# A gated cross-attention layer with experts: the shared part of the last twelve token tiles as six further experts in products of quarters

## The chip, the cores and the metric

The kernel runs on one core of a Trainium2 chip, in one launch. The metric is the time of an execution in microseconds of device time; before the change it is 3289.31 us, the median of three runs (3281.03 to 3296.91). The profile is that of one further execution. Everything is float32. TensorE (PE in the profile) multiplies, VectorE (DVE) and ScalarE (ACT) empty its PSUM banks and compute elementwise, GpSimd (POOL) computes elementwise and issues gathers and scatters, and SyncE (SP) issues nearly all other transfers.

## The reference, cut to what matters

There are 8 x 512 = 4096 tokens of width 1024, which the kernel takes as 32 tiles of 128 rows.

```python
x = x + tanh(g_xattn) * mlstm(layernorm(x), ctx, ctx, ...)        # 16 heads, causal
y = layernorm(x)
logits = y @ router_w.T                                           # 16 experts
w, idx = top_k(softmax(logits), 2);  w = w / sum(w)
shared = (silu(y @ shared_gate_w) * (y @ shared_up_w)) @ shared_down_w      # hidden width 1024
routed[t] = sum over t's two experts of w * ((silu(y @ gate_w[e]) * (y @ up_w[e])) @ down_w[e])   # hidden width 512
out = x + tanh(g_ffn) * (shared + routed)
```

Every token goes through the shared part, and through two of the sixteen experts.

## The kernel before, in words

The order of the work is the program's: a build step places the instructions on each engine, near the order in which they are written but moved where operands are ready, and each engine then runs its own list strictly in order, waiting on semaphores. SP's list is one of these: a transfer that has to wait for its buffer holds back all that stand behind it.

**Attention, with shared units beside it.** A loop over the 32 tiles (the second half of `flamingo_layer`, from `for i in range(1, NT)`) computes attention for tile i, prepares tile i+1 and finishes tile i-1. `finish_rows` (L663) stores the new row x1 and its layer norm y to DRAM, `turn_rows` (L671) stores y transposed (`yT_d`) and queues the shared part of finished tiles as units. `shared_units` (L218) makes them: eight `chunk` units (L247; a chunk is 128 hidden columns, gate and up, weights streamed by `stream`, 1 MB per chunk), then for each tile two `project_down` units (L269). The first six tiles (SINGLE) are queued one by one, 128 columns per matmul and half the cost of a unit in a chunk; tiles 6 to 25 in pairs, 256 columns. `fill` (L207) pops units at four fixed places of each step, and a fifth time in steps 1 to 27. The result, x1 plus tanh(g) times the shared part, goes to `base_d`.

**Routing.** Each tile's two experts and its places in their lists are found beside attention. After the last tile a chain of small DVE operations orders the experts and makes the lists of tokens (`tok_i`, `row_i`), whereupon POOL gathers the first rows and SP loads the first weights. A branch on the number of overflowing tokens follows (L1123 and L1124; every engine reads the number there).

**Experts.** For each expert (loop over `e`), 512 rows, in ten of them 64 more. Both projections are done in quarters: two by two blocks of weights and rows, seven products in place of eight (the Winograd form), with sums of weights by POOL (`weight_sums`, L1134, four operations of 128 x 512 for a step), sums of rows by DVE (`token_sums`, L1101), and the quarters put together by DVE and ACT as they are read out of PSUM (`Step`, L1168). Each expert has four steps (gate and up, two each), in which `down_sums` (L1207) lets POOL prepare the down weights, and two halves of the down projection (`down_tiles`, L1218), before which DVE forms sums of the hidden values (hsum). The results are scaled by ACT and scattered to `routed_d`, two rows per token. Weights lie in a pool of four buffers (`wts`): `load_hidden` (L1054) and `load_down` (L1065) take a buffer when the matmuls of its last user are through. Six PSUM banks rotate under the products (`bank`, L1153). A pool of five buffers (`gat`) holds gathered rows.

**Tail.** After the last expert the shared part of tiles 26 to 31 is done as three pairs of plain units, with the weights held in SBUF, and beside it POOL adds up all outputs: `combine` (L1296) loads the two routed rows and the base of a tile, adds them with two POOL operations of 128 x 1024 (`add_routed`, L1271), and issues the store itself. For the six last tiles the routed rows are added to x1 first, and DVE adds the shared part half by half and SP stores it (L278, L1302).

Of the kernel before, what the change touches and what calls it, by code (L numbers as in the profile page):

```python
# [35 lines left out]
LAST = 3  # L36
SINGLE = 6
SPARE = 4
SLOTS = 5
# [3 lines left out]
def flamingo_layer(  # L43
# [151 lines left out]
    class Unit:  # L195
        def __init__(self, run, load=None, cost=1.0):
            self.run, self.load, self.cost = run, load, cost
            self.also = None
# [7 lines left out]

    def fill(n: float = 1):  # L207
        while n > 0 and units:
            unit = units.popleft()
            n -= unit.cost  # L210
            unit.ready()
            for k in range(min(2, len(units))):
                units[k].ready()
            unit.run()
            if unit.also is not None:
                unit.also()

    def shared_units(pools, tiles, gate_up, down, store, more=None, near=None):  # L218


# [3 lines left out]

        def new(kind, shape):
            pool, tag, bufs = pools[kind]
            return pool.tile(shape, F32, tag=tag, name="sh_" + kind, bufs=bufs)

        def load_y():
# [3 lines left out]
            st["yT"] = new("yT", [P, NC, 2 * P])  # L233
# [5 lines left out]
        def load_chunk(k: int):  # L239
            if k == 0:  # L240
                load_y()
            st[k] = gate_up(k)
            if k == 2 and more is not None:
                for t in range(len(tiles)):
                    load_row(t)

        def chunk(k: int):  # L247
            if k == 0:
                st["hT"] = new("hT", [P, 2 * NFC, 2 * P])
# [8 lines left out]
            act = new("act", [P, 2 * P])  # L258
# [3 lines left out]
        def load_row(t: int):  # L262
            if ("row", t) not in st:
                st["row", t] = new("base", [P, D])
                nc.sync.dma_start(st["row", t], x1_d[tiles[t]])
                if more is not None:
                    more(tiles[t], st["row", t])

        def project_down(t: int, half: int):  # L269
            cols = slice(half * 512, (half + 1) * 512)  # L270
            po = ps.tile([P, 512], F32, tag="o", name="pso")
            for k in range(2 * NFC):
                nc.tensor.matmul(  # L273
                    po, lhsT=st["hT"][:, k, t * P : (t + 1) * P], rhs=down(k)[:, cols],
# [4 lines left out]
            store(tiles[t], row, half)  # L279
# [22 lines left out]

    sh_pools = {"yT": (sh, "yT2", 2), "hT": (sh, "hT2", 1), "base": (sh, "base", 2), "act": (sh, "act", 2)}

    def keep_base(i: int, row, half: int):
        if half == 1:
            nc.sync.dma_start(base_d[i], row)
# [5 lines left out]
    with ExitStack() as actx:  # L313
# [357 lines left out]
        def turn_rows(i: int):  # L671
# [8 lines left out]
            if (alone or i % 2 == 1) and i < NT - 2 * LAST:  # L680
                tiles = [i] if alone else [i - 1, i]
                near = yT if i == 0 else None
                units.extend(shared_units(sh_pools, tiles, stream, lambda k: sh_down[:, k, :], keep_base, near=near))
# [89 lines left out]
        prep_norm(2)  # L773
        for i in range(1, NT):
            nxt, last, back = i + 1 < NT, i % NS == NS - 1, i > 1
            if nxt:
                prep_queries(i + 1)
                prep_keys(i + 1)
# [3 lines left out]
            fill()  # L782
# [9 lines left out]
            fill()  # L792
# [6 lines left out]
            fill()  # L799
# [12 lines left out]
            fill()  # L812
# [6 lines left out]
            if i < NT - SPARE:  # L819
                fill(SLOTS - 4)  # L820
# [205 lines left out]

    NQ = NC // 2
# [26 lines left out]
    def load_hidden(n: int, pool=wts):  # L1054

        e = n // 2
        if e < NE:
            w = (gate_w, up_w)[n % 2][of_expert(e)].rearrange("o (c p) f -> p (o c) f", p=P)
        else:
            fs = slice((e - NE) * F, (e - NE + 1) * F)  # L1060
            w = (sh_gate_w, sh_up_w)[n % 2][:, fs].rearrange("(c p) f -> p c f", p=P)
        ws[n] = pool.tile([P, NC, F], F32, tag="w", name="w")
        nc.sync.dma_start(ws[n], w)

    def load_down(e: int, pool=wts, tag="w"):  # L1065
        wdn[e] = pool.tile([P, NFC, D], F32, tag=tag, name="wd")
        if e < NE:
            w = down_w[of_expert(e)].rearrange("o (c p) d -> p (o c) d", p=P)
        else:
            w = sh_down_w[(e - NE) * F : (e - NE + 1) * F, :].rearrange("(c p) d -> p c d", p=P)  # L1070
# [29 lines left out]

    def token_sums(e: int):  # L1101
        if e >= NE:
            return
# [10 lines left out]

    fill(len(units) + 1)
    streamed.close()
    tk = ctx.enter_context(tc.tile_pool(name="tk", bufs=1))
    for k in range(NM + 1):
        transpose_rows(0, k)
    token_sums(0)  # L1120
# [8 lines left out]
    hidden = ExitStack()  # L1129
    hd = hidden.enter_context(tc.tile_pool(name="hid", bufs=2, side="right"))  # L1130

    sums: dict = {}

    def weight_sums(g: int):  # L1134

        n, i = g // 2, g % 2
        if n >= 2 * NE:
            return
        w = ws[n]
        a11, a12, a21, a22 = (  # L1140
            w[:, q * NQ : (q + 1) * NQ, (2 * f + i) * P : (2 * f + i + 1) * P] for f in range(2) for q in range(2)
        )
        tile_ = hd.tile([P, 3, NQ, P], F32, tag="s", name="wsum", bufs=2)
        s1, s2, s4 = (tile_[:, k] for k in range(3))
        nc.gpsimd.tensor_tensor(s1, a21, a22, ALU.add)  # L1145
        nc.gpsimd.tensor_tensor(s2, s1, a11, ALU.subtract)  # L1146
        nc.gpsimd.tensor_tensor(a21, a11, a21, ALU.subtract)
        nc.gpsimd.tensor_tensor(s4, a12, s2, ALU.subtract)
        sums[g] = [a11, a12, s4, a22, s1, s2, a21]
# [68 lines left out]
    def down_tiles(e: int, i: int):  # L1218
# [31 lines left out]
        for t in (1, 0):  # L1250
            j = e * NM + i + 2 * t
# [16 lines left out]
    routed = routed_d[0 : 2 * T, :].rearrange("(k t) d -> t k d", k=2)  # L1268
    combined = 0

    def add_routed(i: int, row=None):  # L1271

        nonlocal combined
        if combined % 3 == 2:
            rows = [gt_.tile([P, D], F32, tag="gat", name="sum") for _ in range(3 if row is None else 2)]
            parts = rows[:2]
            for k in range(2):
                nc.sync.dma_start(parts[k], routed[i * P : (i + 1) * P, k, :])
        else:
            if combined % 3 == 0:  # L1280
                t = tk.tile([P, 3, NQ, WIDE // 2], F32, tag="t", name="sums")
                rows = t.rearrange("p k c n -> p (k c n)")[:, : 3 * D].rearrange("p (k d) -> p k d", d=D)
            else:
                rows = tl_[0].tile([P, 3, D], F32, tag="rows", name="sums")
            parts = [rows[:, k, :] for k in range(2)]
            nc.sync.dma_start(rows[:, 0:2, :], routed[i * P : (i + 1) * P])
            rows = [rows[:, k, :] for k in range(3)]
        combined += 1
        if row is None:
            row = rows[2]  # L1290
            nc.sync.dma_start(row, base_d[i])
        for part in parts:
            nc.gpsimd.tensor_tensor(row, row, part, ALU.add)
        return row

    def combine(i: int):  # L1296
        row = add_routed(i)
        nc.gpsimd.dma_start(out_rows[i * P : (i + 1) * P, :], row)

    def store_half(i: int, row, half: int):  # L1300
        cols = slice(half * 512, (half + 1) * 512)
        nc.sync.dma_start(out_rows[i * P : (i + 1) * P, cols], row[:, cols])  # L1302

    def held(k: int):
        cols = slice(k % NFC * P, (k % NFC + 1) * P)
        return tuple(ws[2 * (NE + k // NFC) + n][:, :, cols] for n in range(2))

    tl_ = []
    pools = {"yT": (mx_, "xT", 2), "hT": (mv_, "hT", 1), "base": (mv_, "yo", 3)}
    pairs = [  # L1310
# [80 lines left out]
```

## Time and profile before

| | |
|---|---|
| the profiled execution | 3280.16 us, of which the span of its instructions is 3278.4 us |
| median of three runs | 3289.31 us |
| attention with units | 0 to some 1676 us |
| experts 0 to 15 | 1692.8 to 3026.4 us; with rest rows 85.6 to 86.5 us each, without 76.8, the last 72.5 |
| tail | 3026.4 to 3278.4 us |
| TensorE clock granted | 0.985 on average |
| DMA | 567.55 MB, 173 GB/s on average; 299 GB/s in the tail |

A line of instructions reads: line, engine, operation, output and inputs, shapes, count, then busy time, mean of one in ns, and how long the engine was idle just before these and what ended that. A float32 product of TensorE is two instructions, and the recorded durations of a stream of matmuls overlap, so it is the busy time that adds up. In the list of transfers the last number is the median time from issue to landing.

### The profile page before, as it was taken

What the parts mean: (1) busy time and instruction counts of PE and PEld (TensorE: products, weight loads), DVE (VectorE), ACT (ScalarE), POOL (GpSimd) and SP (SyncE); (2) the same over time, 40 slices, a digit from 0 to 9 for tenths busy, and PEclk for the clock granted to TensorE, in tenths of its full rate; (3) what the DMA queues carried; (4) which work ended last, traced back from release to release, by engine and by line L of the source; (5) the groups of instructions that cost most, each with busy time, mean ns of one, the idle gap of its engine ahead of it and who ended that gap; (6) DMA issues with size and microseconds to landing.
All of it is one profiled execution on the core that took longest, in us unless ns stands there. A gap on an engine that the chain in (4) does not pass through costs nothing. (4 is left out here: it accounts for less than half of the span.)

```text
span 3278.4 us, 44195 instructions
## 1 busy us (share of the span) xinstructions
PE 3190.7 (97%) x17043; PEld 2367.7 (72%) x17043; DVE 1673.5 (51%) x3779; ACT 884.9 (27%) x1830; POOL 1173.9 (36%) x904
## 2 busy tenths in 40 slices
PE   6899999999999999999979999999999999999999
PEld 5788778777877867877846666666666777777776
DVE  5646665566675676667534444444444455543000
ACT  3433443434434434434211111111111111111000
POOL 2211111212111111112145554555555555542685
PEclk8899989999999999999989999999999999999999
DMA  6688776556655655655553333333333343334896
GB/s 199 180 229 256 225 207 185 179 169 180 199 162 174 200 169 173 187 168 168 161 188 113 119 128 136 128 132 132 126 117 127 133 152 137 122 124 143 330 346 223
DMA packets 456680, 567.55 MB, mean 173 GB/s; under 512 B 24016, under 2 KB 343424, under 8 KB 452496
## 3 DMA queue, kind: packets, MB, share of 16 engines
q1 hardware_dynamic: 426784, 477.83, 45.9%
q0 software_dynamic: 26064, 86.04, 7.2%
q8 instruction: 137, 2.24, 0.3%
q10 hardware_dynamic: 3616, 0.79, 0.1%
q14 instruction: 79, 0.65, 0.1%
HBM read 447.72 MB, written 116.88 MB: 172 GB/s over the span
## 5 line engine op out<-in xcount | busy, mean ns | idle before, releaser
L1162 PE MATMUL pq<-xT,w 128*128 128x288 f32 (+1 forms) x1536 | 381.7, 399 | 9.9 <-DVEq L1124 9.9
L254 PE MATMUL pgu<-sh_yT,swg 128*128 128x256 f32 (+1 forms) x1920 | 380.6, 350 | 4.2 <-DMA swg<-L_ffn_shared_gate_w_dram 3.3
L273 PE MATMUL pso<-sh_down,sh_hT 128*128 128x512 f32 x832 | 371.8, 598 | 1.3 <-DVE sh_hT L260 1.3
L254 PE MATMUL pgu<-sh_yT,swu 128*128 128x256 f32 (+1 forms) x1920 | 367.6, 344 | 1.9 <-DMA swu<-n_L_ffn_shared_up_w_dram 1.9
L1162 PEld LDWEIGHTS pq<-xT,w 128*128 128x128 f32 x1536 | 292.7, 191 | 85.7 <-issue 20.7
L254 PEld LDWEIGHTS pgu<-sh_yT,swu 128*128 128x128 f32 x1920 | 317.9, 191 | 35.6 <-DMA swu<-n_L_ffn_shared_up_w_dram 2.5
L254 PEld LDWEIGHTS pgu<-sh_yT,swg 128*128 128x128 f32 x1920 | 311.7, 191 | 40.5 <-DMA swg<-L_ffn_shared_gate_w_dram 2.3
L113 POOL TENSOR_SCALAR ve<-bmv 128x1 f32<-128x1 f32 x64 | 15.6, 243 | 782.6 <-DVE bmv L125 782.6
L273 PEld LDWEIGHTS pso<-sh_down,sh_hT 128*128 128x128 f32 x832 | 153.4, 190 | 174.1 <-issue 167.1
L1162 PE MATMUL pq<-tsum,wsum 128*128 128x288 f32 (+1 forms) x1024 | 261.2, 398 | 12.5 <-POOL wsum L1146 12.5
L260 DVE TENSOR_TENSOR sh_hT<-sh_act,pgu 128x256 f32<-128x256 f32 (+1 forms) x152 | 56.8, 375 | 389.5 <-ACT sh_act L259 389.1
L1162 PEld LDWEIGHTS pq<-tsum,wsum 128*128 128x128 f32 x1024 | 192.1, 191 | 52.9 <-POOL wsum L1146 12.9
L1186 DVE TENSOR_TENSOR hT<-pq,u 128x288 f32<-128x288 f32 (+1 forms) x128 | 57.0, 445 | 275.2 <-PE pq L1162 254.9
L541 POOL TENSOR_SCALAR_AFFINE_SELECT d<-d 128x2048 f32<-128x2048 f32 x31 | 62.9, 2028 | 351.5 <-DMA d<-nm_d 294.7
L259 ACT ACTIVATE sh_act<-pgu 128x256 f32<-128x256 f32 (+1 forms) x152 | 53.3, 351 | 488.9 <-PE pgu L254 481.1
L254 PE MATMUL pgu<-sh_yT,w 128*128 128x256 f32 x768 | 166.2, 379 | 0.0
L1145 POOL TENSOR_TENSOR wsum<-w 128x512 f32<-128x512 f32 x64 | 82.5, 1290 | 225.4 <-PE pq L1162 208.3
L254 PEld LDWEIGHTS pgu<-sh_yT,w 128*128 128x128 f32 x768 | 145.9, 190 | 21.1 <-issue 1.4
L565 ACT ACTIVATE d<-d,cols 128x128 f32<-128x128 f32 x496 | 149.9, 388 | 40.0 <-DVE cols L526 24.3
L1252 ACT ACTIVATE yo<-yo,wslot 128x1024 f32<-128x1024 f32 x64 | 73.5, 1149 | 294.3 <-DVE yo L1237 294.3
L1098 ACT COPY xT<-ptx 128x512 f32<-128x512 f32 (+1 forms) x74 | 41.2, 557 | 393.9 <-PE ptx L1095 386.3
L601 PE MATMUL pav<-v,d 128*128 128x65 f32 x1024 | 142.6, 270 | 1.6 <-ACT sq L607 1.6
(266 smaller groups left out, 5711.3 us busy)
## 6 DMA issues: line engine op xcount, KB each, us to landing
swg<-L_ffn_shared_gate_w_dram SPq DMA_DIRECT2D x128, 512.0 KB, 4.6
swu<-n_L_ffn_shared_up_w_dram SPq DMA_DIRECT2D x128, 512.0 KB, 5.1
w<-in_L_ffn_gate_w_dram SPq DMA_DIRECT2D x16, 2048.0 KB, 10.7
w<-in_L_ffn_up_w_dram SPq DMA_DIRECT2D x16, 2048.0 KB, 9.2
wd<-in_L_ffn_down_w_dram SPq DMA_DIRECT2D x16, 2048.0 KB, 7.8
d<-nm_d SPq DMA_DIRECT2D x31, 1024.0 KB, 6.0
sums<-routed_d SPq DMA_DIRECT2D x22, 1024.0 KB, 6.2
x_sb<-in_x_dram SPq DMA_DIRECT2D x32, 512.0 KB, 5.1
```

Of the source, the lines that this page charges most:

```text
L254: nc.tensor.matmul(pg[:, half, :n], lhsT=w[:, c, :], rhs=st["yT"][:, c, :n], start=(c == 0), stop=(c == NC - 1),)
L259: nc.scalar.activation(act[:, :n], pg[:, 0, :n], AF.Silu)
L260: nc.vector.tensor_mul(st["hT"][:, k, :n], act[:, :n], pg[:, 1, :n])
L273: nc.tensor.matmul(po, lhsT=st["hT"][:, k, t * P : (t + 1) * P], rhs=down(k)[:, cols], start=(k == 0), stop=(k == 2 * NFC - 1),)
L541: nc.gpsimd.affine_select(out=q.d, in_=q.d, compare_op=ALU.is_ge, fill=NEG, base=0, pattern=[[0, NH], [1, P]], channel_multiplier=-1,)
L565: nc.scalar.activation(q.d[:, h, :], q.d[:, h, :], AF.Exp, bias=q.cols[:, 0, h : h + 1])
L601: nc.tensor.matmul(pav[:, 2 * k + hh, :], lhsT=q.d[:, h, :], rhs=q.v[:, h, :], start=first, stop=first or hh == 1,)
L1098: copy(dst[:, half * 4 : half * 4 + 4, :], pt[:, :, cols])
L1145: nc.gpsimd.tensor_tensor(s1, a21, a22, ALU.add)
L1162: nc.tensor.matmul(out, lhsT=left[:, c, :], rhs=right[:, c, :], start=(c == 0), stop=(c == chunks - 1))
L1186: nc.vector.tensor_tensor(out, part, other, ALU.add)
L1252: nc.scalar.activation(rows[t], rows[t], AF.Copy, scale=wslot.pop(j))
```

## The change

`HELD = 3` groups of four tiles (20 to 31) are held back from the units beside attention. Their shared part, 1024 hidden columns, becomes two jobs of 512 for each group, and these six jobs follow the sixteen experts in the same loop (`JOBS = 22`), with the same products of quarters: rows come from `yT_d` by plain loads (`load_rows`) in place of gathers and transposes, the second job of a group uses the sums of the first, and the result is added by DVE to a held tile of four rows (`add_shared`) instead of being scattered; after the second job SP stores it. The three pairs of the tail are gone. The adding up that POOL did beside the tail now stands in the jobs (`sums_beside`): in the first job of each group the routed rows are added to the x1 rows of its four tiles, and the twenty other tiles are combined one at a time; one of the two adds of each tile is DVE's now, the other POOL's, and the parts and the row of a combine lie in the five `gat` buffers.

Beside attention there are 20 tiles for 26, the first two alone, the others in pairs. `fill` carries over what it owes: it runs units while something is owed, at four places of a step, 0.75 of a unit at each in steps 1 to 4 and `each` = 99 / 108 of a unit afterwards, so that 8 units are left for the end of the stage. `weight_sums(0)` is moved ahead of the branch, and `token_sums(0)` behind it.

```diff
-LAST = 3
-SINGLE = 6
-SPARE = 4
-SLOTS = 5
+HELD = 3
+SINGLE = 2
+RESERVE = 8
+FIRST = 4
...
+    owed = 0.0
+
     def fill(n: float = 1):
-        while n > 0 and units:
+        nonlocal owed
+        owed += n
+        while owed > 1e-6 and units:
             unit = units.popleft()
-            n -= unit.cost
+            owed -= unit.cost
...
             alone = i < SINGLE
-            if (alone or i % 2 == 1) and i < NT - 2 * LAST:
+            if (alone or i % 2 == 1) and i < NT - 4 * HELD:
...
+        each = (6 * (NT - 4 * HELD) - 1 - 3 * FIRST - RESERVE) / (4 * (NT - 1 - FIRST))
         for i in range(1, NT):
+            share = 0.75 if i <= FIRST else each
...
-            fill()
+            fill(share)
...
-            if i < NT - SPARE:
-                fill(SLOTS - 4)
...
+    JOBS = NE + 2 * HELD
...
+    def load_rows(q: int):
+
+        x = columns(NE + 2 * q)
+        for t in range(NM):
+            nc.sync.dma_start(
+                x[:, :, t * P : (t + 1) * P], yT_d[held_tile(q, t)].rearrange("p (c t) -> p c t", t=P)
+            )
...
     def token_sums(e: int):
-        if e >= NE:
+        if e >= JOBS:
+            return
+        if e > NE and (e - NE) % 2 == 1:
+            xTs[e, "b"] = xTs[e - 1, "b"]
             return
...
+    weight_sums(0)
     for k in range(NM + 1):
         transpose_rows(0, k)
-    token_sums(0)
     early.close()

     nov = nc.values_load(nov_i, min_val=0, max_val=2 * T)
...
+    token_sums(0)
...
         for t in (1, 0):
+            if e >= NE:
+                add_shared(e, i + 2 * t, rows[t])
+                continue
...
+    def add_routed(i: int, row, base):
+
+        nc.sync.dma_start(row, base[i])
+        for k in range(2):
+            part = gt_.tile([P, D], F32, tag="gat", name="part")
+            nc.sync.dma_start(part, routed_d[k * T + i * P : k * T + (i + 1) * P, :])
+            (nc.vector, nc.gpsimd)[k].tensor_tensor(row, row, part, ALU.add)

     def combine(i: int):
-        row = add_routed(i)
+        row = gt_.tile([P, D], F32, tag="gat", name="row")
+        add_routed(i, row, base_d)
         nc.gpsimd.dma_start(out_rows[i * P : (i + 1) * P, :], row)
...
+    def add_shared(e: int, t: int, part):
+
+        q, half = (e - NE) // 2, (e - NE) % 2
+        row = xTs[NE + 2 * q, "sum"][:, t, :]
+        nc.vector.scalar_tensor_tensor(row, part, tgf, row, ALU.mult, ALU.add)
+        if half == 1:
+            i = held_tile(q, t)
+            nc.sync.dma_start(out_rows[i * P : (i + 1) * P, :], row)
+
+    todo = deque(range(NT - NM * HELD))
+
+    def sums_beside(e: int, k: int):
+
+        if e < NE:
+            return
+        if (e - NE) % 2 == 0 and k < 4:
+            if k == 0:
+                xTs[e, "sum"] = mx_.tile([P, NM, D], F32, tag="xT", name="held")
+            add_routed(held_tile((e - NE) // 2, k), xTs[e, "sum"][:, k, :], x1_d)
+        elif todo:
+            combine(todo.popleft())
+
+    for e in range(JOBS):
+        q = (e + 1 - NE) // 2 if e + 1 >= NE and (e + 1 - NE) % 2 == 0 and e + 1 < JOBS else None
+        if q == 0:
+            load_rows(q)
         for k in range(4):
...
             step.finish()
+            sums_beside(e, k)
+        if q:
+            load_rows(q)
         load_down(e + 1)
...
         down_tiles(e, 0)
         token_sums(e + 1)
-        if e == NE - 1:
-            pairs[0][0].ready()
+        sums_beside(e, 4)
         down_tiles(e, 1)
...
         load_hidden(2 * e + 4)
-
-    hidden.close()
...
-    for pair in pairs:
-        units.extend(pair)
...
-    while units:
-        fill()
-        while todo and len(todo) * n > (len(units) - 6) * (NT - 2 * LAST):
-            combine(todo.popleft())
+        if e < JOBS - 1:
+            sums_beside(e, 5)
```

## The prediction

> **What bounds the kernel now.** I read the busy shares first, then the groups by shape, then windows cut at the stage borders, then TensorE's waits, then the DMA landings.
>
> ```profile
> span 3278.4 us, 44195 instructions
> ...
> PE 3190.7 (97%) x17043; PEld 2367.7 (72%) x17043; DVE 1673.5 (51%) x3779; ACT 884.9 (27%) x1830; POOL 1173.9 (36%) x904
> ```
>
> TensorE is busy for all but 87.7 us, so the span is TensorE's work plus those gaps. The work that the change touches, by shape:
>
> ```profile
> L273 PE MATMUL pso<-sh_down,sh_hT 128*128 128x512 f32 x832 | 371.8, 598 | 1.3 <-DVE sh_hT L260 1.3
> ...
> L254 PE MATMUL pgu<-sh_yT,swg 128*128 128x256 f32 x1280 | 301.0, 386 | 0.0
> ...
> L254 PE MATMUL pgu<-sh_yT,swu 128*128 128x256 f32 x1280 | 289.3, 379 | 0.0
> ...
> L254 PE MATMUL pgu<-sh_yT,w 128*128 128x256 f32 x768 | 166.2, 379 | 0.0
> ...
> L254 PE MATMUL pgu<-sh_yT,swg 128*128 128x128 f32 x640 | 79.5, 277 | 4.2 <-DMA swg<-L_ffn_shared_gate_w_dram 3.3 <-DMA sh_yT<-yT_d 0.8
> L254 PE MATMUL pgu<-sh_yT,swu 128*128 128x128 f32 x640 | 78.3, 275 | 1.9 <-DMA swu<-n_L_ffn_shared_up_w_dram 1.9
> ...
> L273 PE MATMUL pso<-wd,sh_hT 128*128 128x512 f32 x192 | 82.9, 592 | 0.0
> ```
>
> Busy time over count is what an instruction costs in a stream (a float32 product is two instructions): 0.231 us for 256 columns beside attention, 0.216 in the tail, 0.123 for 128 columns, 0.447 and 0.432 for 512. The means (379 and more) overlap and don't add. The windows are attention steps 20 to 27, steps 28 and 29, experts 14 and 15, and the tail:
>
> ```profile
> 1058.30:1461.00 402.70, 399.83 (x2537) 304.32 (x2536) 257.17 (x652) 164.55 (x354) 75.46 (x62) 1.00 0.58 178
> 1461.00:1546.20 85.20, 84.84 (x601) 67.27 (x600) 59.67 (x148) 36.63 (x81) 18.59 (x16) 1.00 0.58 180
> ...
> 2877.10:2953.90 76.80, 76.44 (x313) 56.34 (x312) 38.68 (x66) 12.73 (x23) 34.20 (x25) 1.00 0.35 124
> 2953.90:3026.40 72.50, 72.50 (x282) 53.30 (x281) 26.82 (x58) 10.49 (x19) 22.04 (x16) 1.00 0.38 138
> 3026.40:3278.00 251.60, 248.22 (x961) 182.11 (x959) 19.82 (x37) 10.71 (x26) 166.69 (x92) 1.00 0.81 299
> ```
>
> The columns are length, then busy PE, PEld, DVE, ACT, POOL, then clock, DMA share and GB/s. A step with five shared units lasts 50.3 us (402.7 / 8) with DVE busy 32.1; with four units 42.6, and TensorE is still never short (0.36 us idle in two steps). The gaps sit in the first five steps (31.6 us from 18 to 286 us, timeline), in the change from attention to experts (22.4), the rest scattered.
>
> **Work removed and added.** Beside attention four single tiles and one pair go. A single is 256 instructions x 0.123 + 32 x 0.447 = 45.8 us, a pair 256 x 0.231 + 64 x 0.447 = 87.7: 4 x 45.8 + 87.7 = 271 us. In the tail three pairs go: 166.2 + 82.9 = 249. Added are six jobs of 512 rows and 512 hidden columns in seven products instead of eight. Expert 15 is such a job exactly (no rest rows, no transposes for a follower): 72.5 us, all busy; 56 x 0.216 = 12.1 per step, four steps 48.5, then 24 of down products. 6 x 72.5 = 435. TensorE's work: 435 - 520 = **-85 us**. All of it was on the path. Weight loads (191 ns) lie under products of 0.216, so they cost nothing. ScalarE is at 14% in expert 15 and loses the scaling of rows in the jobs: nothing.
>
> **Attention with fewer units.** From step 5 on, 11 units stand where 12 slots are; fill runs one whenever something is owed, so each third step has three units, with the slot between the second scores and the values empty, and two have four. The four-unit step is in the trace: no new idle. A three-unit step has 14.2 us of attention and 3 x 7.1 of units, 35.6 us, against 32 of DVE plus what DVE waits for in any case (row<-rstd alone 30.4 us in 17 steps, 1.8 each): nearly level, and DVE is in order. I take 3 us of idle in each of nine such steps and 0.6 in the other eighteen, 38, against 15 now: **+20**. Bounds: 0 (DVE catches up in the longer steps) and +66 (3 us in every step). In the first four steps the units fall from 5 to 3 while the clock is half at times: **+5**, bounds 0 and 15.
>
> **From attention to experts.**
>
> ```profile
> PE pq L1162 <- POOL wsum L1146: 12.5, 1, 12.5
> PE pq L1162 <- DVEq L1124: 9.9, 1, 9.9
> ```
>
> After the last routing product (pw at 1656.3 us) TensorE had 46 down instructions as cover; the built program of the changed kernel has 62, so 16 x 0.44 = 7 us more. The first weight sums now stand before the branch at L1124 on POOL; SP passes the branch only when its 8 MB of weights are issued (SP took 11.5 and 12.6 us at two issues), which doesn't change, and the token sums now stand behind it on DVE, 1.4 us for the first: 2.5 us won of 12.5. **-9.5**, bounds -18 and 0.
>
> **The adds inside the jobs.** This part speaks against the change. In the tail POOL did all adds (2.35 us each) and TensorE, DVE and ACT waited for none of it. Now each of 32 tiles has one add on DVE (1.22 us, by the row of L661 of that shape) and one on POOL, and the built order puts them among DVE's evictions and POOL's weight sums. It doesn't spread them: jobs 16 and 18 get four held tiles and eight combines each, job 20 four and four, odd jobs none. Queued behind a waiting DVE add are evictions, hence PSUM banks and the hidden values of the down products; behind a waiting POOL add, the next weight sums. Five buffers carry rows and parts: the first part of combine n+2 takes the row buffer of combine n, so SP issues it when that row's store has landed, and everything behind it on SP waits too.
>
> ```profile
> x_sb<-in_x_dram SPq DMA_DIRECT2D x32, 512.0 KB, 5.1
> ...
> sum<-routed_d SPq DMA_DIRECT2D x20, 512.0 KB, 9.9
> ...
> out_dram<-sums POOLq DMA_DIRECT2D x17, 512.0 KB, 5.2
> ...
> out_dram<-sum POOLq DMA_DIRECT2D x9, 512.0 KB, 7.6
> ```
>
> With 5 us a load and 5.2 a store, from job 16's start (0): the fourth held part gets a buffer after POOL's first held add at 20 and lands at 25; DVE adds it by 26, POOL by 28.6; then weight sums (4 x 1.3) to 34, combine 0's POOL add to 36.3, its store lands at 42, combine 2's part at 47, DVE's add done at 48.2, where three evictions of step 3 have waited since 40. Combine 1's POOL add stands behind further weight sums: 44.3; stored 50; combine 3's part 55; DVE's add 56. It stands before the last evictions of step 3 and the hidden sums (4.3 us): the down products start at 60.3 instead of 48.5, **12 us late**. Combines 4 to 7 then stay just ahead. Jobs 18 and 20 have the same order around combines 2 and 3.
>
> Here the Trainium skill (DMA: Bandwidth & Descriptors, Anatomy of one DMA) prices a POOL-issued DMA at about 2.0 us plus bytes over 436 GB/s: 3.2 us for 512 KB. The row says 5.2. With 3.2 for stores and loads the same walk ends 7 us late; with the loaded pair 9.9 and 7.6, 24 late at combine 3 and 42 by the job's end, as combines 6 and 7 are then late too. Job 16 moves 26 MB, some 300 GB/s, as much as the tail's 299, but its loads are one or two at a time, not in threes as the tail's: I stay nearest the 5 us rows, with 13 a job.
>
> A second rule speaks against gaps like these: TensorE: Matmul & The Clock Gate (Why this matters for your kernels) says that an idle gap over about 3 us brings the half clock back. The trace, after the first gap:
>
> ```profile
> 1692.84 5.85 PE L1162 MATMUL pq<-xT,w 128*128 128x288 f32 x16 [9.94 <-DVEq L1124]
> ...
> 1724.61 4.04 PE L1162 MATMUL pq<-xT,w 128*128 128x288 f32 x16
> ```
>
> 1.8 us lost at this gap; after the other, 2.1 more (8 instructions in 4.21 against 2.10). The rule's single 3.4 us window at half rate would be 1.7. I take 2. So 3 x (13 + 2) = **+45**, bounds 27 and 117.
>
> **The end.** Now one DVE eviction (0.75) and a 256 KB store follow the last product. Then: an eviction, two scaled adds of 1024 (1.3 each) and 512 KB: **+4**, bounds 3 and 8.
>
> **Sum.** -85 + 20 + 5 - 9.5 + 45 + 4 = -20.5. The profiled execution took 3280.2 us (span 3278.4), so 3259.7. The median of the runs, 3289.3, lies 9 above it; I put the forecast half-way, at 3264.
>
> **Rivals.** (a) The adds hardly wait: loads and stores near 3 us (shortest landings 2.6 and 2.0): 7 + 2 a pair of jobs, 27 instead of 45, and attention keeps up: 3222 to 3245. For: one load at a time. Against: the medians. (b) Slower: the chain store, load, DVE add, POOL add, store in jobs 16, 18 and 20 becomes the bound, as loads take 9.9 and stores 7.6: 42 + 42 + 24 + 9 = 117, 3280 - 65.5 + 117 = 3332. It decides from 22 us a pair of jobs on, where -65.5 is used up. For: 26 MB in a job, weights of 2 MB in the same queue. Against: at such latencies the job moves only 230 GB/s, so there's no load to cause them. (c) Attention becomes bound by DVE, 3 us idle in each step: +66 for +20, about 3306. Against: the four-unit steps. That the products would not shrink is excluded: their number is in the built program.
>
> **Chances.** My case 0.45 (3240 to 3285), (a) 0.2, (b) 0.22, (c) 0.13. One half of a per cent, 16 us, is about what a measurement of this kernel can tell from no change. Faster by more: 0.25 of my case and (a), 0.45; within: 0.25; slower: (b) and part of (c), 0.30. The range 3222 to 3335 takes in (a) and most of (b).
>
> **What would show it.** Right: steps of 36 and 43 us; jobs of 72.5 us in 17, 19, 21 and some 85 in 16 and 18; DVE adds waiting for DMA there, TensorE for hidden sums after step 3, half clock behind. Wrong: jobs 16 and 18 alike to 17 (a), or over 100 (b); DVE without idle time in attention (c). The forecast falls if POOL's weight sums, not DVE, stop TensorE, or if odd jobs wait.

## The result, and the profile after

The median after the change is 3304.3 us (20 runs, 3287.8 to 3313.2), against 3286.9 us before (20 runs beside them, 3279.6 to 3302.8). The ratio is 1.0046, with a 95% interval of 1.0032 to 1.0060: the change costs half a per cent. The forecast was 3264, faster by 0.8%. The profiled execution of the changed kernel has a span of 3286.1 us, 7.7 more than before.

The busy shares, from the page of the changed kernel:

```profile
PE 3137.3 (95%) x16291; PEld 2299.7 (70%) x16291; DVE 1944.0 (59%) x4107; ACT 880.4 (27%) x1838; POOL 1291.4 (39%) x986
```

TensorE did 53.4 us less work (3190.7 before) where 85 less were forecast, and it stood idle for 148.8 us instead of 87.7. The span grew by the difference. So work went and idle time took its place; the question is where.

The windows answer it by stage: eight attention steps (20 to 27), expert 15, jobs 16, 17 and 21. Columns as before: length, busy PE, PEld, DVE, ACT, POOL, then clock, DMA share, GB/s.

```profile
893.20:1231.00 337.80, 326.70 (x2233) 245.99 (x2232) 250.93 (x643) 150.76 (x328) 71.16 (x62) 1.00 0.58 177
...
2719.70:2793.30 73.60, 72.69 (x282) 53.12 (x281) 35.90 (x62) 10.41 (x19) 33.97 (x25) 1.00 0.39 143
2793.30:2883.80 90.50, 75.42 (x282) 53.24 (x280) 53.67 (x69) 7.10 (x16) 63.53 (x39) 0.94 0.81 284
2883.80:2962.70 78.90, 74.80 (x280) 54.00 (x281) 50.35 (x71) 5.86 (x14) 35.92 (x25) 0.98 0.53 188
...
3206.70:3279.20 72.50, 72.50 (x281) 53.01 (x279) 33.98 (x63) 6.00 (x14) 19.82 (x12) 1.00 0.04 15
```

The jobs behave much as forecast: the last one, with no adds beside it, takes 72.5 us and is all busy; 16 and 17 take 90.5 and 78.9 (18 and 20, not shown, 85.4 and 84.9). Attention is where the forecast was missed. In these eight steps TensorE idles 11.1 us, where before it idled 2.9, and a step lasts 42.2 us on average. Its waits between the fifth step and the last values (us in total, times, longest), against 7.4 us at the first of these places before and none at the second:

```profile
PE pt L394 <- ACT qT L395: 21.7, 16, 3.1
PE pt L394 <- DVE count L698: 9.5, 13, 2.5
```

Set against each other by stage (us of the two profiled executions; a step begins with its first scores):

| stage | before | after | difference | forecast |
|---|---|---|---|---|
| start to step 5: busy / idle | 241.9 / 43.7 | 188.4 / 49.6 | -47.6 | |
| step 5 to the last values: busy / idle | 1322.2 / 14.6 | 1121.3 / 38.6 | -176.9 | |
| last values to the experts: busy / idle | 59.1 / 11.3 | 66.1 / 9.8 | +5.5 | |
| **start to the experts** | 1692.8 | 1473.8 | **-219.0** | -246.0 |
| experts 0 to 15 | 1333.6 | 1319.5 | -14.1 | -9.5 |
| **jobs, for the tail's pairs** | 248.2 | 485.9 | **+237.7** | +231 |
| after the last product | 3.8 | 6.9 | +3.1 | +4 |
| **sum** | 3278.4 | 3286.1 | **+7.7** | -20.5 |

The forecast column puts -271 + 20 + 5 in the first stages, the gap's -9.5 with expert 0, and 435 + 45 - 249 in the jobs. About 22 us of the 28 that were missed lie ahead of the jobs. Up to the experts the forecast was missed by 27 us, of which 23.6 are work: TensorE's busy time fell there by 247.4 us, where 271 were put down. Its idle time rose by 28.4 us there, where 25 were.

The medians differ by more than the profiles, 17 us against 7.7. The profiled execution of the changed kernel is the fastest of its 20, 16.5 us under their median; that of the kernel before lies 6.8 us under its own. So the table compares two fast executions, and in which stage the other 10 us arise no trace shows. The clock is a candidate: over an execution it was 0.975 to 0.985 in the changed kernel, highest in the profiled one. The start of the program is not the reason, although the clock column differs there. The first 60 us of before and of after show

```profile
0.00:60.00 60.00, 30.57 (x245) 26.18 (x245) 30.34 (x71) 17.94 (x44) 15.24 (x38) 0.78 0.64 183
```

```profile
0.00:60.00 60.00, 31.10 (x245) 26.60 (x245) 30.15 (x71) 17.95 (x44) 15.17 (x37) 0.96 0.64 181
```

By the column the same 245 instructions ran at a mean clock of 0.78 in the one and 0.96 in the other, and yet they took the same time: the next one begins at 61.4 us before and at 61.6 after. So the column can be wrong at the start of a trace, and times are compared here. Single executions do differ in their start: in a profile of a kernel with the same attention (`weight_sums(0)` called behind the branch, below) step 5 came at 249.9 us instead of 238.0.

### The profile page after: what moved, and what is told of

The parts are those of the page before. It is cut to its first block, busy times and chain, and to the rows that moved or that the text cites. A ratio compares the mean times of both kernels' runs of the same rounds, so it can differ in the third digit from the quotient of the medians.

```text
span 3286.1 us, 43283 instructions
## 1 busy us (share of the span) xinstructions
PE 3137.3 (95%) x16291; PEld 2299.7 (70%) x16291; DVE 1944.0 (59%) x4107; ACT 880.4 (27%) x1838; POOL 1291.4 (39%) x986
## 4 chain that ended last, share of the span: by engine, by line
PE 45%; DVE 4%; DMA 3%; issue 1%; POOL 1%; DVEq 0%; POOLq 0%; SPq 0%
PE pq L1169 43%; DMA part<-routed_d 2%; PE ptx L1087 2%; PE pq L1270 1%; DVE hsum L1233 1%; DVE hT L1191 1%; DVE row L1285 0%; DMA out_dram<-held 0%; DMA out_dram<-row 0%; POOL held L1285 0%; DVE hsum L1234 0%; DVE held L1285 0%; DMA held<-x_d 0%; DVE up L1190 0%; POOL row L1285 0%
## 5 line engine op out<-in xcount | busy, mean ns | idle before, releaser
L1169 PE MATMUL pq<-xT,w 128*128 128x256 f32 (+1 forms) x2112 | 514.1, 393 | 11.9 <-DVEq L1150 8.4
L1169 PEld LDWEIGHTS pq<-xT,w 128*128 128x128 f32 x2112 | 401.5, 191 | 106.2 <-issue 13.0
L1169 PE MATMUL pq<-tsum,wsum 128*128 128x256 f32 (+1 forms) x1408 | 351.0, 392 | 3.2 <-DVE u L1255 3.2
L248 PE MATMUL pgu<-sh_yT,swg 128*128 128x256 f32 (+1 forms) x1280 | 289.7, 376 | 1.1 <-DMA swg<-L_ffn_shared_gate_w_dram 1.1
L248 PEld LDWEIGHTS pgu<-sh_yT,swg 128*128 128x128 f32 x1280 | 227.9, 192 | 31.4 <-DVE sh_hT L254 1.3
L1169 PE MATMUL pq<-wd,hT 128*128 128x512 f32 x352 | 172.4, 605 | 33.4 <-DVE hT L1191 31.9
L1169 PE MATMUL pq<-xT,wsum 128*128 128x256 f32 (+1 forms) x704 | 175.5, 392 | 0.0
L1169 PE MATMUL pq<-tsum,w 128*128 128x256 f32 (+1 forms) x704 | 174.9, 391 | 0.0
L1169 PE MATMUL pq<-dsum,hT 128*128 128x512 f32 x352 | 166.3, 593 | 3.8 <-DVE hT L1191 3.2
L1169 PE MATMUL pq<-dsum,hsum 128*128 128x512 f32 x352 | 167.3, 598 | 0.0
L1244 DVE TENSOR_TENSOR yo<-pq,u 128x512 f32<-128x512 f32 x176 | 119.6, 686 | 70.0 <-PE pq L1169 56.3
```

The costliest lines, as they stand in the source:

```text
L248: nc.tensor.matmul(pg[:, half, :n], lhsT=w[:, c, :], rhs=st["yT"][:, c, :n], start=(c == 0), stop=(c == NC - 1),)
L1169: nc.tensor.matmul(out, lhsT=left[:, c, :], rhs=right[:, c, :], start=(c == 0), stop=(c == chunks - 1))
L1244: nc.vector.tensor_tensor(rows[t][:, halves[half]], part, other, ALU.add)
```

## The experiments

The theory after the result: the loss has two parts. In the jobs DVE, in order, waits for parts that have not landed (as forecast). In attention a unit taken away doesn't return its own time, since something else in the step becomes late. Rivals: the jobs lose by something other than the adds; the idle time in attention comes of the grain of whole units; the gap at the experts, not attention, is mis-sized.

**The price of the adds.** The kernel leaves out the loads of the routed parts and their adds; base rows are still loaded and stored.

```diff
     def add_routed(i: int, row, base):
         nc.sync.dma_start(row, base[i])
-        for k in range(2):
-            part = gt_.tile([P, D], F32, tag="gat", name="part")
-            nc.sync.dma_start(part, routed_d[k * T + i * P : k * T + (i + 1) * P, :])
-            (nc.vector, nc.gpsimd)[k].tensor_tensor(row, row, part, ALU.add)
```

> Leaves out the loads of the routed parts and their adds in all six jobs (the outputs lack the routed rows); base rows are still loaded and stored. Theory of the forecast (the adds cost the jobs some 50 us, DVE waiting for parts): the six jobs fall from 485.9 us to 435 to 442, the profiled span from 3286 to about 3238, the ratio to the kernel before about 0.990. Rival (the jobs lose by something else: row loads, weight sums, weights not landed in time): jobs 16, 18 and 20 stay at 80 us or more. Either way attention must stay as it is in the changed kernel: the first product of the experts at about 1474 us and 28 us more idle time of TensorE than before.

Measured: ratio 0.9922 (0.9909 to 0.9934). All six jobs in one window:

```profile
2807.70:3248.00 440.30, 435.73 (x1681) 318.55 (x1679) 231.48 (x379) 37.35 (x86) 179.58 (x114) 1.00 0.31 105
```

440.3 us for 485.9, busy for 435.7, and the work of a job is the forecast's 72.6 each. So nothing but the parts and their adds made the jobs longer, 45.6 us. The experts began at 1480.0, 6 us later than in the changed kernel, and took 8 us longer, in code that the edit leaves alone; so the profiled span, 3254.4 us, lies 16 above the expected one. How the adds cost time can be seen in the changed kernel's job 16, in DVE's list and then TensorE's:

```profile
2835.24 2.29 DVE L1285 TENSOR_TENSOR row<-row,part 128x1024 f32<-128x1024 f32 x1 [3.22 <-DMA part<-routed_d]
...
2853.50 2.27 DVE L1285 TENSOR_TENSOR row<-row,part 128x1024 f32<-128x1024 f32 x1 [5.80 <-POOL wsum L1135]
```

```profile
2861.04 2.07 PE L1169 MATMUL pq<-wd,hT 128*128 128x512 f32 x2 [11.31 <-DVE hT L1191]
```

DVE stands before an add until its part has landed. At the second of these adds the profile names POOL, but a part landed at 2853.31 us, just ahead of it, and SP had issued that part at 2849.52, when a store by POOL had landed (2849.50). The last evictions of the gate and up products and the sums of hidden values come behind this add, and TensorE waits 11.3 us for them in the down products. The forecast's walk had 12 us at this very place. The two instructions behind the gap then take 2.07 us; two of the same shape ahead of it took 1.12.

**Whose add waits.** Both adds of each tile on POOL, order as it comes: `nc.gpsimd` for `(nc.vector, nc.gpsimd)[k]`.

> The changed kernel with both adds of each tile on POOL and the order left as it comes. If the loss is DVE standing in order behind parts that have not landed: the jobs fall from 485.9 us to 445 to 460, since POOL is busy for 20 to 35 us of a job without adds. Rival (it is the order without spread that costs, whichever engine waits: behind a waiting add on POOL stand the next weight sums, which TensorE needs every 12 us): 470 us or more, TensorE waiting for weight sums in jobs 16, 18 and 20.

Measured: ratio 1.0072 (1.0052 to 1.0092), the jobs 493.2 us. The rival's figure. TensorE's waits in the jobs:

```profile
PE pq L1169 <- DVE hT L1191: 24.3, 5, 9.0
PE pq L1169 <- POOL wsum L1135: 18.8, 3, 12.3
```

The first theory fails: without any add on DVE the jobs became no shorter. Some of the wait moved with the adds, since TensorE now waits for weight sums that stand behind adds on POOL. But it still waits for DVE, 24.3 us, although DVE has no add left and before the longest of these waits does not stand still. Its own operations had become longer. Two neighbours from its list there:

```profile
3037.22 0.42 DVE L1190 TENSOR_TENSOR up<-pq,u 128x256 f32<-128x256 f32 x1
3037.68 5.96 DVE L1191 TENSOR_TENSOR hT<-hT,up 128x256 f32<-128x256 f32 x1
```

In this execution the operation hT<-hT,up of 128x256, which reads SBUF alone, took 0.42 us in the 47 cases with no POOL arithmetic beside it, and 1.46 on average in the 48 where POOL worked for over 60% of its time. The one that reads a PSUM bank, up<-pq,u, took 0.42 in both. In the kernel before it was 0.42 against 1.06, and 0.42 in both. Counted against their time alone, DVE's operations on hidden values lost 31 us in the changed kernel's six jobs and its adds 30; in this run the former lost 83. So the adds cost in two ways: work that waits for memory stands in front of work that TensorE needs, and POOL's arithmetic slows DVE's. How the changed kernel's 45.6 us divide between the two was not tested.

**The order.** The same adds, each tile's written one slot behind its loads and tied behind that slot's last eviction (DVE) and last down sum (POOL), which also spreads them over all six jobs:

```diff
+        parts = [gt_.tile([P, D], F32, tag="gat", name="part") for _ in range(2)]
+        return lambda: [(nc.vector, nc.gpsimd)[k].tensor_tensor(row, row, parts[k], ALU.add) for k in range(2)]
...
+        while late:
+            with tc.issue_after(last["DVE"]), tc.issue_after(last["POOL"]):
+                late.popleft()()
...
-            combine(todo.popleft())
+            late.append(combine(todo.popleft()))
```

> The same loads and adds, but each tile's two adds are written one slot later than its loads, and tied behind the last eviction of that slot on DVE and the last down sum on POOL. Theory (DVE and POOL stand in order and wait for parts that haven't landed; the bytes are no limit): the jobs come to 438 to 450 us, 36 to 48 less, with hardly a wait of DVE for parts, the ratio to the kernel before about 0.993. Rival (the loads and stores themselves are the limit at some 280 GB/s, so that adds wait wherever they stand): less than 15 us are won. Attention unchanged.

Measured: ratio 0.9949 (0.9931 to 0.9968). The jobs take 461.1 us, 24.8 less, short of the 36 to 48 expected: DVE's waits for parts fell from 39.0 us to 1.9, but TensorE waits 12.9 us, in five places, for DVE between the two halves of the down products. The bytes are no limit, as the rival would have it: 219 GB/s over the six jobs. The run changes two things at once, the order and the spread: no job gets more than six tiles' adds, where in the changed kernel jobs 16 and 18 get eleven. The run with two groups held, below, bears on which of them won.

**Is that last wait the add's?** Both adds go to POOL in the two slots of the down products.

```diff
-                late.popleft()()
+                late.popleft()((nc.vector if k < 4 else nc.gpsimd, nc.gpsimd))
```

> As the lagged kernel, but in the two slots of the down products both adds are POOL's. In the lagged kernel TensorE waits 12.9 us in five places between the two halves of the down products for DVE, which has a tile's add (1.2 us) and the sums of rows before it, and the half clock follows for 3.4 us each time. If the add is the cause: 8 to 15 us less than the lagged kernel, jobs 16 to 20 at 73 to 75.5 us. If the sums of rows or the scaled adds are: no change within 3 us.

Measured: ratio 0.9987 (0.9978 to 0.9996); jobs 461.9 us, and the same wait 16.6 us. So the add is not its main cause. Three of the five places fell from 2.1 to 1.4 us each, but the two longest, between an odd job's halves, grew to 6.0 and 6.3. There DVE stands before the sums of rows for the next job, whose rows have not landed:

```profile
DVE tsum L1115 <- DMA xT<-yT_d: 17.1, 2, 8.7
```

In the lagged kernel it waited 3.0 us for these. This kernel came out 0.4% slower than the lagged one. Its profile has 12.2 us more (3272.7 for 3260.5 us of span), 0.8 of them in the jobs and 12.0 ahead of the experts, where the edit changes nothing. To see whether the lagged kernel's own ratio holds, it was run again:

> The lagged kernel once more, beside the next two on one chip: its ratio to the kernel before was 0.9949, the variant with the late adds on POOL gave 0.9987, though the job stages of both took 461 to 462 us in their profiles. If that difference is one of the place of the half clock in single executions, the lagged kernel now comes to 0.995 to 0.999; if it was real, to 0.993 to 0.997.

Measured: 0.9951 (0.9931 to 0.9970). It holds (its experts begin at 1481.5 in the profile, against 1484.8 in the mixed kernel and 1472.8 in the first run); what the mixed kernel loses outside the jobs stays open.

**The gap at the experts.** The call of `weight_sums(0)` is written behind the branch again.

> The first weight sums go back behind the branch, all else as in the changed kernel. If it is their move that took expert 0 from 102.9 to 87.9 us: expert 0 comes to 100 to 103 and the time rises by 13 to 15 us. If it is the longer cover by units (64 down instructions in place of 46): expert 0 stays below 90 and the time does not change by more than 3 us.

Measured: ratio 1.0059 (1.0043 to 1.0075), which can't be told from the changed kernel's; expert 0 at 87.4 us. But the run does not show what it was made for. The branch is L1149 in this kernel, and POOL's list has the sums still ahead of it:

```profile
1485.48 2.48 POOL L1134 TENSOR_TENSOR wsum<-w 128x512 f32<-128x512 f32 x2
...
1504.23 6.43 POOL L1223 TENSOR_TENSOR dsum<-wd 128x1024 f32<-128x1024 f32 x2 [2.29 <-DVEq L1149]
```

The build step had moved them there. In the kernel before they stand behind it, and POOL waits for SP first:

```profile
1707.38 2.49 POOL L1145 TENSOR_TENSOR wsum<-w 128x512 f32<-128x512 f32 x2 [16.60 <-SPq L1124]
```

So in both kernels in which the sums stand ahead of POOL's branch, TensorE's wait of 12.5 us for them is gone. That this is due to their place is likely, but no run has put them back. The longer cover by units can be read for itself: from the last values to the experts TensorE is busy 7.0 us longer and idle only 1.5 less.

**The grain.** Each unit in two of half the cost, eight matmuls of gate or up, or four of the down products.

```diff
-        us = [Unit(lambda k=k: chunk(k), lambda k=k: load_chunk(k), cost) for k in range(2 * NFC)]
+        us = []
+        for k in range(2 * NFC):
+            us.append(Unit(lambda k=k: chunk(k, 0), lambda k=k: load_chunk(k), cost / 2))
+            us.append(Unit(lambda k=k: chunk(k, 1), None, cost / 2))
```

> Each unit beside attention is split into two of half the cost (gate and up; four and four of the down products), so that no place of a step stays empty. Rival theory of the grain (the idle time in attention comes from places that whole units leave empty): idle time in steps 5 to 31 falls from 39 us to 10 to 15, the experts begin 25 us or more earlier than in the changed kernel. Theory of the chain (DVE, ACT and POOL need their time between the products of a step, and with 92 units of work less this time is not covered wherever the units stand): the experts begin less than 10 us earlier, and the short products of attention stay at the higher busy time.

Measured: ratio 1.0028 (1.0019 to 1.0037), which can't be told from the changed kernel's 1.0046 (1.0032 to 1.0060). In the profile the experts begin at 1487.0, later, not 25 us earlier, and idle time in steps 5 to 31 is 47.7 us. The grain is out. The largest wait is again one at the transposes, for DVE's count: 29.0 us in 17 times.

**What a unit returns.** Two kernels with far fewer units, for the length of a step alone: `HELD = 7` and `HELD = 5` in the lagged kernel.

> Seven groups held, so only four tiles (32 units) are left beside attention: 0.03 units at a place from step 5 on, and fourteen jobs behind the experts. Only the lengths of steps 5 to 30 are asked. In the kernel before a step with five units lasts 50.6 us, in the changed one 44.8 with four and 39.0 with three, so a unit taken away has returned 5.8 us of its 7.2. If the chain of DVE, ACT and POOL through a step sets a floor, a step without units stays at 29 to 34 us, twice TensorE's 14 to 16. If each unit simply costs 5.8 us by itself, it falls to 22 us.

> Five groups held: twelve tiles beside attention, 1.9 units a step from step 5 on, ten jobs behind the experts, adds one slot late as in the lagged kernel. Floor of some 31 us: steps of 33 to 36 us, TensorE idle 4 us or more in each. Straight line of 5.8 us a unit: 32.5 us and under 2 us idle. The job stage itself: ten jobs of 73 to 78 us; the whole, by the price of 5.8 us against 6.0 to 6.4 in a job (a job of four tiles' half is worth twelve units), slower than the lagged kernel with three groups by 30 us or more.

The lengths of steps 5 to 30, grouped by the units in them (a unit counted as 7.2 us of its matmuls), means in us:

| kernel | units | steps | length | TensorE idle | TensorE busy outside units |
|---|---|---|---|---|---|
| before | 5 | 20 | 50.6 | 0.4 | 14.2 |
| before | 4 | 4 | 43.7 | 0.8 | 13.9 |
| changed | 4 | 16 | 44.8 | 1.4 | 14.5 |
| changed | 3 | 9 | 39.0 | 1.8 | 15.2 |
| five groups held | 2.7 | 14 | 38.2 | 3.3 | 15.2 |
| five groups held | 2 | 8 | 31.4 | 2.5 | 14.4 |
| seven groups held | 0 | 20 | 39.7 | 12.7 | 27.0 |

Each of the last two kernels was executed once. Down to two units the lengths stay near the straight line (31.4 us with two units, where the line gave 32.5 and the floor 33 to 36), but the idle time of 2.5 us lies between the two theories (under 2 and over 4). A step without units is as long as one with three, more than either theory had it; the window of one such step, a long one (step 20 of the kernel with seven groups held), says why:

```profile
815.40:863.50 48.10, 28.75 (x210) 23.75 (x209) 31.22 (x96) 17.66 (x44) 9.76 (x8) 0.61 0.24 84
```

The clock is at 0.61 on average: the short products of attention take nearly twice their time, 27.0 us for 14 to 15, and even DVE is busy for less than two thirds of this step (for 28.7 of 39.7 us on average). So units beside attention do two things: they are work themselves, and where there are at least two in a step TensorE's clock stays high (0.97 on average in the eight steps with two). The executions took 3740.8 us and, with five groups, 3377.1: far slower, as the second expectation had it.

**The other way.** Two groups held, 24 tiles beside attention, four jobs, in the lagged kernel (up to two tiles' adds in a slot).

> Two groups held in place of three: 24 tiles beside attention (4.6 units a step), four jobs, the adds one slot late, two tiles' adds in some slots. If a unit beside attention costs 5.8 us at this load, four tiles more cost 24 x 5.8 = 139 us there, and two jobs fewer save 2 x 77 = 154: 15 us less than the lagged kernel (3262), less up to 20 for adds that stand closer (eight tiles a job for 5.3): ratio to the kernel before 0.990 to 0.997. Rival (units cost their full 7.2, as the forecast had it): 173 against 154, 19 us slower than the lagged kernel, ratio 1.000 or more.

Measured: ratio 1.0009 (0.9997 to 1.0022), missing the range. The experts begin 160 us later than in the changed kernel, of which some 12 lie before step 5 (a start at 0.74 of the clock); 148 / 24 is 6.2 us a unit, neither 5.8 nor 7.2. The four jobs take 332.8 us, so two jobs fewer save 128, not 154: with eight tiles' adds a job DVE waits 39.6 us for parts again, and job 17 takes 98.3 us. The price of a unit was nearly right; the denser adds ate the gain. This also bears on the lagged kernel: here the order is the same, and jobs 17 and 18, with ten and nine tiles' adds, lose 25.8 and 11.1 us against the bare 72.5, as much as the changed kernel's jobs with eight to eleven (12.4 to 18.0). So what the lagged kernel won may be due to the spread as much as to the order; the two were not tested apart.

**What becomes late in a step.** All transposes, ranks and small products of attention take turns in two PSUM banks (tag tr), while the two of the units' down products (tag o) are used by one unit in three. The second half of each transpose and the ranks get those, in the lagged kernel:

```diff
-                pt = ps.tile([P, 4, P], F32, tag="tr", name="pt")
+                pt = ps.tile([P, 4, P], F32, tag=("tr", "o")[half], name="pt")
...
-            pn = ps.tile([P, 2, NE], F32, tag="tr", name="pn")
+            pn = ps.tile([P, 2, NE], F32, tag="o", name="pn")
```

> The lagged kernel with another place in PSUM for some small results of attention: the second half of each group of transposes, and the ranks of the routing, take banks of the tag that the down products of the shared units use (o), in place of the two banks (tr) that all transposes and small products share. TensorE's waits for ACT's copy of qT (24.5 us in 17 times) and for DVE's count (11.3 in 13) stand at transposes, so they may be waits for one of those two banks. If so: idle time in steps 5 to 31 falls from 39 to 10 or 15 us, steps of three and four units to 37.5 and 43.5, the experts begin 30 us earlier, ratio 0.9 per cent below that of the lagged kernel. Rival (the floor of the step is the chain of DVE, and the wait moves to its next link): less than 8 us.

Measured: ratio 0.9879 (0.9858 to 0.9900), 0.7% below the lagged kernel on the same chip. The experts begin at 1455.0 us instead of 1481.5, and idle time in steps 5 to 31 falls from 40.0 to 28.0. TensorE's largest waits in that stage:

```profile
PE pt L394 <- DVE sh_base L269: 4.4, 5, 2.3
PE pt L394 <- DVE rows L452: 4.2, 4, 2.1
PE pt L394 <- DVE count L698: 3.2, 4, 1.4
```

The wait of transposes for ACT's copy is gone from the list and that for the count is a third. So most of them were waits for a bank that an earlier result still filled. Idle time fell less than expected, but busy time fell too (steps of four units: 44.0 us with 14.3 of attention, for 45.3 with 14.7). Was that there before the change?

> The kernel before the change with the same other place for the transposes and the ranks in PSUM. If the waits for the two shared banks come up only where fewer units stand between them (the kernel before has 14 us of idle time in steps 5 to 31): at most 8 us are won, ratio 0.998 to 1.000. Rival (they cost as much before the change, hidden in busy time): 20 us or more, ratio 0.994 or less, and then the step's price of a unit is no matter of these banks.

Measured, the same edit in the kernel before: ratio 0.9982 (0.9973 to 0.9992), about 6 us where the lagged kernel won 24. Most of these waits therefore come with the change: with five units in a step a bank is mostly empty again by the time that it is needed (7.4 us of such waits, not 31.2). The lagged kernel with the other banks is the fastest of all, 1.2% below the kernel before and 1.0% (0.9879 / 0.9982) below the kernel before with the same banks.

## Why the prediction was wrong, point by point

- **Work removed and added: here it failed.** "TensorE's work: 435 - 520 = -85 us. All of it was on the path." The jobs' 435 and the tail's 249 are right (435.7 without the adds; 248.2). The 271 us beside attention are not: TensorE's busy time ahead of the experts fell by 247.4. The 271 were built from busy time per instruction in separate rows, which overlap at their borders; taken together, without counting any moment twice, the units' busy time fell by 252.2. Against that, attention's own products grew by 4.7 us: the short ones take longer as units go (14.2, 14.5, 15.2 us a step); why is not shown. With the idle time below, taking 271 us of units away brought the experts forward by 219.
- **The step lengths.** "The four-unit step is in the trace: no new idle." It was read from two steps near the end of the stage (42.6 us). Sixteen such steps now take 44.8 us, idle 1.4 in each. With its 0.6 of idle the forecast had 43.2, so these steps alone are 26 us longer than forecast. For three units 35.6 and 3 of idle were put down, and 39.0 came. The idle time of steps 5 to 31 was forecast at 38 and is 38.6, by luck of the shares: less than thought in the three-unit steps, more in the four-unit ones. (38 against 15 before is +23, and the forecast wrote +20; it rose by 24.0.) In all a unit taken away returned 5.8 us of its 7.2.
- **What the price of 5.8 means.** A job does the work of twelve units. Beside attention those returned 12 x 5.8 = 70 us by the step lengths, and 73 by the whole stage (219.0 for the three jobs' worth of six tiles); a job costs 72.5 bare and 81 on average with its adds (485.9 / 6). So the six tiles taken from attention could win nothing, although TensorE's work shrank. Only the tail's could: twelve units took 83 us there (249 / 3), more than a bare job, and hardly more than one with its adds. The forecast priced both moves by TensorE's work.
- **First steps: right.** +5 forecast, 5.9 measured (idle 43.7 to 49.6 before step 5).
- **The gap at the experts: right in sign, larger, and the two reasons changed places.** -9.5 forecast; the first gap shrank by 1.5 us and expert 0 by 15.0. The longer cover was put at 7 us and took 1.5 from the gap. The moved sums were put at 2.5 of the 12.5 us that TensorE had waited for them, and the whole wait is gone, with the slow products behind it (likely by the place of the sums, which no run put back). Nor were both of SP's long issues weights: the one of 12.6 us stored base rows (`base_d<-sh_base`).
- **The adds: mechanism right in part, size nearly.** +45 forecast, 50.9 measured (485.9 - 435), of which the parts and adds account for 45.6. The jobs 16, 18 and 20 lost 18.0, 12.9 and 12.4 us where 15 each was put down; the odd job 17 lost 6.4, and waits in odd jobs had been named as a sign against the forecast. That DVE's operations become longer beside POOL's is not in the forecast at all: its adds were put at 1.22 us, and the 20 that POOL worked through took 2.59 on average. Landings were 4.8 us for parts and 5.5 for stores, near the 5 and 5.2 taken, and not the 3.2 of the fit by the Trainium skill.
- **The end: right.** +4, measured 3.1.
- **The rivals.** Rival (b) is refuted: loads did not become the bound. Rival (c), attention bound by DVE at +66, was nearer than its 0.13: attention lost 52 us of the 271 (271 - 219.0) where the forecast allowed 25. But DVE is busy for only 31 us of 42 in a step, and other banks brought the experts forward by 26.5 us, half of that loss.

In short, jobs and end came within 6 us of the forecast; attention missed it by 27, 23.6 of them work that TensorE did not save, and that made a gain into a loss.

## What to carry to other kernels

Work that fills the waits of another stage is not worth its own time when it is taken out: measure what a step returns per unit, over many steps, before it is moved to a place where each unit costs its full price. When filler goes, look for what it had kept apart, here results that share two PSUM banks. And what waits for memory must not stand ahead of the work that the bounding engine needs: load in one slot, add in a later one, and spread such work thinly. Last, moving a call in the source need not move the instruction: look for it in the list of its engine.

## What was unexpected of the hardware

TensorE's clock depends on how the gaps fall, not only on their length. In the changed kernel a gap of 3.12 us (up to 730.5 us) was followed by one stretch at half rate, and a gap of 2.50 us (up to 466.2) by none:

```profile
731.00:735.00 4.00, 4.00 (x32) 3.08 (x34) 2.72 (x6) 0.39 (x1) 0.79 (x2) 0.59 0.33 133
...
468.00:476.00 8.00, 8.00 (x38) 3.85 (x40) 8.00 (x21) 4.89 (x12) 0.00 (x0) 1.00 0.52 153
```

In the kernel before, a gap of only 1.60 us sufficed (up to 470.4 us):

```profile
468.00:471.40 3.40, 1.80 (x14) 1.66 (x14) 1.44 (x4) 3.31 (x8) 0.00 (x0) 0.93 0.43 161
471.40:474.80 3.40, 3.40 (x37) 2.59 (x36) 0.88 (x5) 0.93 (x3) 0.00 (x0) 0.50 0.95 349
```

The half clock lasted 17 us, all through the short products that followed, and ended once a unit's stream had begun. The rule of the prediction, half clock after gaps of over about 3 us, fits the first two and not the third. The Trainium skill (TensorE: Matmul & The Clock Gate, What's actually happening) says that TensorE's activity is judged in windows of 3413 ns that run free of the program. That leaves room for all three if a window can count as idle with some work in it; no run here varied the phase or tested this.

DVE and POOL are not independent either: hT<-hT,up, which reads SBUF alone, took 0.42 us by itself and 1.0 to 1.5 on average beside POOL's arithmetic in five of the kernels, up to 5.96 with both adds on POOL.
